# Cross attention in a transformer layer: where a tile's value products stand between two tiles' scores

## The chip, the core and the metric

The kernel runs on one core of a Trainium2 chip. The metric is the device time of one execution in microseconds (us). The core's engines are named as the profile names them: PE is TensorE (PEld its weight loads), DVE is VectorE, ACT is ScalarE, POOL is GpSimd, SP is SyncE, which issues the DMAs. Each engine runs its instructions in the order in which the program issues them, and waits on semaphores for the others.

## The reference, cut to what matters

One encoder layer over a short context (77 rows) and one decoder layer over 2048 rows, for two batches, width 512, 16 heads of 32. The change lies in the decoder's cross attention:

```
y = y + _mha(yn, yn, ...)                              # self attention over 2048 rows
q = _ln(y, n2) @ wq.T + bq                             # cross attention
scores = einsum('bhqd,bhkd->bhqk', q, k) / sqrt(hd) + bias
attn = softmax(scores, axis=-1)                        # 77 keys
out = einsum('bhqk,bhkd->bhqd', attn, v)               # the value products
y = y + out @ w_out.T + b_out
h = _ln(y, n3)
y = y + relu(h @ ff1.T + b1) @ ff2.T + b2              # feed-forward
```

All in float32.

## The kernel before, in words

The 2 x 2048 rows are cut into eight blocks of 512 rows, and each block into four tiles of 128 rows (`t` = 0 to 3). Self attention comes first, for all blocks, with the encoder and the cross attention of block 0 laid into it. Then come the feed-forward parts of the eight blocks; while block x is in its feed-forward part, block x + 1 goes through its cross attention. So seven cross attentions (`cross(x)`, line 1462, x = 1 to 7) run inside feed-forward parts, each with four tiles.

A feed-forward part has `per` = 56 slots. `ff_slot` (line 1439) is one slot's worth of it: in slots 0 to 27 a piece of the first product (`first_product`, line 1366, matmuls at line 1376), in slots 28 to 55 a piece of the second (`second_product`, line 1396, matmuls at line 1405). Both are Strassen-Winograd forms: seven products in place of eight, with sums of quarters made on DVE and POOL (`sums_h`, line 1333, which uses `half_sum`, line 1322, and `minus`, line 1112). `first_product` hands its result to DVE (line 1389, or to ACT at 1386) and then to ACT for the relu (line 1392).

The cross attention is a plan: a list of 56 lists of pieces, filled in `cross`. The main loop (lines 1659 to 1665) takes for each slot first the pieces of the plan, in the order in which they were put in the list (`next(side)`), and then `ff_slot`. The schedule is manual: the order on each engine is the order of the calls.

For tile t the plan has, counted from slot 13 + 5t, the stages of `attend_stages` (line 796):

- `score` (matmuls at line 808, +0): 16 small products, four heads in each of four PSUM banks, and behind them eight DVE operations, for each bank a maximum (line 817) and a subtraction (line 818);
- `exp` on ACT (line 821, +2), `sums` on DVE (lines 826, 827, +3), `normalize` on POOL (line 832, +3);
- `turned` (+7): four groups of transposes on PE (line 838), each into a bank of its own, and four copies on ACT (line 839) into `pts`;
- `times_v` (+10), the value products: 16 small matmuls into one bank (line 846) and a copy of that bank by ACT (line 850) into a buffer with the tag `xr`. For tiles 1 and 3 `sums_o` (line 1517) follows at once: three DVE operations, two of them in `minus` (line 1113) and one at line 1522, all of which read the bank of the products itself, and one on POOL.

So `times_v` of tile t falls on slot 23 + 5t, and `score` of tile t + 2 on slot 13 + 5(t + 2), the same one; in the list the products stand first, because the loop over t put them there first. That concerns t = 0 (slot 23) and t = 1 (slot 28); the products of tiles 2 and 3, in slots 33 and 38, meet no score.

The output products (`o_product`, line 1525, matmuls at line 1536) of tiles 0 and 1 lie in slots 31 to 34, those of tiles 2 and 3 in slots 40 to 43 (`O_SLOTS`); they read the copies and the sums. The norms behind them (`norm_stages`, line 759) start at slots 35, 36, 44 and 45, and their transposes (line 783) come four slots later.

PSUM has eight banks. In the feed-forward parts banks 4 to 7 belong to the feed-forward products; all pieces of the cross attention take banks 0 to 3 in a ring (`bank`, line 180, with `banks` = 4): whoever writes a bank waits until its last reader is done. The weights of the feed-forward and of the projections come by DMA through a ring of 16 tiles, filled by `feed` (line 1274) at each slot.

Of the kernel before, what the change touches and what calls it, by code (L numbers as in the profile page):

```python
# [54 lines left out]
def tile_encoder_decoder(ctx: ExitStack, tc: tile.TileContext, ins, out):  # L55
# [103 lines left out]
    with (  # L159
# [597 lines left out]
        def norm_stages(y, n, row, place, done):  # L757

            keep = {}

            def stats():
                st = sm.tile([P, 6], F32, name="bnst", tag="bnst")
                mv = sm.tile([P, 2], F32, name="cmv", tag="cmv", bufs=4)
                rs = sm.tile([P, 3], F32, name="crs", tag="crs", bufs=4)
                nc.vector.bn_stats(st, y())
                nc.vector.bn_aggr(mv, st)
                nc.vector.tensor_scalar_add(rs[:, 0:1], mv[:, 1:2], EPS)
                nc.gpsimd.tensor_tensor(rs[:, 1:2], rs[:, 0:1], mhalf[:, 0:1], ALU.pow)
                nc.gpsimd.tensor_scalar(rs[:, 2:3], mv[:, 0:1], rs[:, 1:2], -1.0, ALU.mult, ALU.mult)
                keep.update(rs=rs)  # L770

            def center():
                xn = keep["xn"] = place()
                rs = keep["rs"]
                nc.scalar.activation(xn, y(), AF.Identity, bias=rs[:, 2:3], scale=rs[:, 1:2])

            def add():
                nc.gpsimd.tensor_tensor(y(), y(), row, ALU.add)

            def turned():  # L780
                xn, pt, dst = keep["xn"], bank(), done()
                for c in range(NC):
                    nc.tensor.transpose(pt[:, ts(c, P)], xn[:, ts(c, P)], ident)  # L783
                for c in range(NC):
                    sc, bi = vec(f"dec_{n}_s", c), vec(f"dec_{n}_b", c)
                    nc.scalar.activation(dst[:, c, :], pt[:, ts(c, P)], AF.Identity, bias=bi, scale=sc)

            return stats, center, turned, add
# [272 lines left out]
        def y_of(x, t):  # L1061
            return ys[x % 3][:, t, :]
# [399 lines left out]
        def cross(x):  # L1462
# [4 lines left out]
            def place(tag):  # L1467
                if tag == "xr":
                    return lambda: sb.tile([P, D], F32, name=tag, tag=tag, bufs=2)
                return next_xt  # L1470

            for t in range(TB):
                fs = norm_stages(
                    lambda t=t: y_of(x, t), "n2", bv, place("xt"), lambda t=t: nT2[:, :, ts(t, P)]
                )
# [41 lines left out]
            def sums_o(t):  # L1517
                s = {n: of_o(t, n) for n in ("S1", "S2", "S3", "S4", "11", "12", "21")}
                a21, a22 = (held["o", t + 1]["bank"][:, ts(c, TOK)] for c in range(2))
                minus(ve, s["S3"], s["11"], a21)  # L1520
                minus(ve, s["S2"], a22, s["S3"])
                ve.tensor_tensor(s["S1"], s["21"], a22, ALU.add)
                minus(gp, s["S4"], s["12"], s["S2"])
# [36 lines left out]
            for t in range(TB):  # L1560
                at = 13 + 5 * t
                y = lambda t=t: y_of(x, t)
                biased = m == 0 and t < 2
                fs = attend_stages(
                    lambda g, t=t: qT[g // 2][:, g % 2, ts(t, P)], kTc, vc[0][:S, :], y, biased, prs[t % 2],
                    lambda g: pts_all[:S, g, :], place("xr"), wbt,
                    bias_1 if biased and t else None,
                )
                held["o", t] = fs[7]
                if t % 2:  # L1570
                    fs = fs[:5] + (lambda t=t, f=fs[5]: [f(), sums_o(t - 1)],)

                for k, f in zip((0, 2, 3, 3, 7, 10), fs):
                    plan[at + k].append(f)
                fs = norm_stages(y, "n3", bo, place("xt"), lambda t=t: nTt[:, :, ts(t, P)])
                at = (35, 36, 44, 45)[t]
                for k, f in zip((0, 2, 4), fs):
                    plan[at + k].append(f)
                rows_later[x * per + 15 + t] = fs[3]
# [60 lines left out]
        late_loads()  # L1640
        count.update(bank=0, banks=4)
        side = cross(1)
        slot(end)
        for s in range(4):
# [14 lines left out]
        for x in range(len(blocks)):  # L1659
            if x:  # L1660
                side = cross(x + 1) if x + 1 < len(blocks) else iter(())
            for n in range(per):
                if x or n >= 8:
                    next(side, None)
                    ff_slot(x * per + n)
# [37 lines left out]
```

## Time and profile before

| what | value |
|---|---|
| median of 3 runs | 2838.91 us (2832.11 to 2840.88) |
| the profiled execution, its own time | 2843.07 us |
| its span, from the first to the last instruction | 2841.2 us |
| mean granted PE clock | 0.989 |
| busy: PE, PEld, DVE, ACT, POOL | 98%, 74%, 65%, 50%, 31% of the span |
| HBM read, written | 309.51 MB, 41.49 MB |

The profile is of one execution. "Busy" is the time in which an engine has at least one instruction under way; matmuls are pipelined, so the end of one lies behind the start of the next, and the length of a group of them is best read from its start to the start of what follows. A float32 matmul shows as two records, so 16 products are x32. "Granted clock" is the share of full speed that PE was given in a stretch. `<-` in brackets names what ended an engine's idle time.

### The profile page before, as it was taken

How to read it: one execution, taken by the hardware profiler on the slowest of the kernel's cores; microseconds unless marked ns; L12 is line 12 of the kernel's file. 1: busy time of each engine (PE TensorE's matmuls, PEld its weight loads, DVE VectorE, ACT ScalarE, POOL GpSimd, SP SyncE). 2: the span in 40 equal slices, each digit the busy share in tenths (PEclk: the TensorE clock that was granted, in tenths of full speed). 3: DMA queues.
4: the chain of work that ended last, by engine and by line, in shares of the span. 5: the costliest groups of instructions: out<-in, count | busy, mean ns of one | idle time of the engine just before them, and what ended most of it. 6: DMA issues, size and time to landing. Idle time of an engine off the chain costs nothing. (4 is left out here: it accounts for less than half of the span.)

```text
span 2841.2 us, 65873 instructions
## 1 busy us (share of the span) xinstructions
PE 2790.7 (98%) x25998; PEld 2098.5 (74%) x25998; DVE 1857.5 (65%) x5360; ACT 1430.7 (50%) x2751; POOL 879.2 (31%) x745
## 2 busy tenths in 40 slices
PE   9999999999999999999999999999999999999998
PEld 5557666666666556666666677898989898989898
DVE  4666587778886577688788894646464645454545
ACT  3544466656665547665656674444434444434331
POOL 0301043300200303122100003364646464646456
PEclk9899999999999999999999999999999999999999
DMA  6414343401112512233301105464648464646475
GB/s 172 125 47 140 117 141 121 146 21 50 35 50 65 141 39 79 80 101 98 106 20 43 46 24 199 152 222 158 218 151 242 147 221 149 221 148 222 138 223 181
DMA packets 281270, 355.30 MB, mean 125 GB/s; under 512 B 37968, under 2 KB 156544, under 8 KB 280834
## 3 DMA queue, kind: packets, MB, share of 16 engines
q1 hardware_dynamic: 280962, 351.10, 39.9%
q8 instruction: 205, 3.36, 0.5%
q14 instruction: 103, 0.84, 0.1%
HBM read 309.51 MB, written 41.49 MB: 124 GB/s over the span
## 5 line engine op out<-in xcount | busy, mean ns | idle before, releaser
L404 ACT ACTIVATE pp<-pp,nm 128x128 f32<-128x128 f32 (+15 forms) x512 | 612.1, 1202 | 234.3 <-DVE nm L399 234.0
L382 DVE TENSOR_SCALAR_CACHE_REDUCE pp<-psum 128x512 f32<-128x512 f32 (+3 forms) x1024 | 559.4, 590 | 65.4 <-PE psum L373 63.6
L427 PEld LDWEIGHTS psum<-ident,pp 128*128 128x128 f32 x4352 | 472.2, 141 | 105.6 <-DVE pp L382 51.9
L427 PE MATMUL psum<-ident,pp 128*128 128x128 f32 x4352 | 533.1, 277 | 6.6 <-ACT pp L404 3.7
L433 ACT COPY pts<-psum 128x512 f32<-128x512 f32 (+3 forms) x592 | 297.0, 575 | 434.4 <-PE psum L427 304.6
L431 DVE COPY pts<-psum 128x512 f32<-128x512 f32 (+2 forms) x544 | 329.9, 659 | 66.1 <-PE psum L427 65.9
L373 PE MATMUL psum<-kT,q 32*128 32x512 f32 (+3 forms) x2560 | 358.8, 576 | 4.9 <-DVE pp L382 2.5
L444 PEld LDWEIGHTS psum<-pts,vv 128*32 128x32 f32 x8704 | 226.2, 110 | 124.7 <-issue 116.8
L1405 PE MATMUL psum<-pp 128*128 128x128 f32 x2560 | 306.7, 277 | 1.9 <-POOL pp L1113 1.6
L1405 PEld LDWEIGHTS psum<-pp 128*128 128x128 f32 x2560 | 299.2, 193 | 7.2 <-POOL pp L1113 2.1
L444 PE MATMUL psum<-pts,vv 128*32 128x128 f32 x8704 | 279.2, 275 | 0.7 <-ACT pts L433 0.5
L1113 POOL TENSOR_TENSOR pp<-pp 128x512 f32<-128x512 f32 x159 | 210.3, 1340 | 112.4 <-DMA pp<-in_dec_ff_wT_dram 50.9
L1376 PE MATMUL psum<-vv,pp 128*128 128x256 f32 x1024 | 243.6, 390 | 0.0
L373 PEld LDWEIGHTS psum<-kT,q 32*128 32x128 f32 x2560 | 124.0, 183 | 141.3 <-issue 91.2
L1376 PEld LDWEIGHTS psum<-vv,pp 128*128 128x128 f32 x1024 | 195.1, 195 | 27.7 <-issue 0.5
L389 DVE CUSTOM_DVE_ANT_0 pp<-psum,bias 128x256 f32<-128x256 f32 (+1 forms) x512 | 195.9, 411 | 16.7 <-PE psum L373 16.6
L1389 DVE TENSOR_TENSOR kT<-kT,psum 128x512 f32<-128x512 f32 x96 | 65.8, 687 | 190.3 <-PE psum L1376 190.1
L1392 ACT ACTIVATE kT<-kT,vecs 128x256 f32<-128x256 f32 x192 | 86.9, 500 | 173.7 <-DVE kT L1389 173.0
L1376 PE MATMUL psum<-nT,pp 128*128 128x256 f32 x768 | 173.9, 380 | 0.0
L286 POOL TENSOR_TENSOR rstd<-rstd,mhalf 128x1 f32<-128x1 f32 x32 | 18.5, 578 | 471.5 <-DVE rstd L285 368.9
L1376 PEld LDWEIGHTS psum<-nT,pp 128*128 128x128 f32 x768 | 145.6, 191 | 19.6 <-issue 0.2
L472 POOL TENSOR_TENSOR oT<-rirows,oT 128x512 f32<-128x512 f32 x30 | 38.7, 1289 | 360.9 <-DMA rirows<-rec 327.2
(207 smaller groups left out, 3816.8 us busy)
## 6 DMA issues: line engine op xcount, KB each, us to landing
pp<-w_d SPq DMA_DIRECT2D x520, 256.0 KB
pp<-in_dec_ff_wT_dram SPq DMA_DIRECT2D x112, 256.0 KB
wqk<-in_dec_sa_in_wT_dram SPq DMA_DIRECT2D x64, 256.0 KB
bias<-tzg SPq DMA_DIRECT2D x128, 128.0 KB
pp<-wo_d SPq DMA_DIRECT2D x56, 256.0 KB
wbig<-in_dec_sa_in_wT_dram SPq DMA_DIRECT2D x8, 1024.0 KB
vv<-in_enc_ff_wT_dram SPq DMA_DIRECT2D x8, 1024.0 KB
wbig<-in_dec_sa_out_wT_dram SPq DMA_DIRECT2D x8, 1024.0 KB
```

The source lines that it names most:

```text
L373: nc.tensor.matmul(banks[r][:, : kn * P], q[rows4(r), ts(t, P)], kT[rows4(r), g, k0 * P : (k0 + kn) * P], start=True, stop=True,)
L382: nc.vector.tensor_scalar(p[:, k0 * P : (k0 + far) * P], s[:, : far * P], 1.0, None, ALU.mult, ALU.max, accum_out=st["mx"][:, r, c : c + 1],)
L389: nc.vector.tensor_tensor_reduce(p[:, (i + 1) * P - w : (i + 1) * P], s[:, far * P : kn * P], biases[b, m, g][:, r, 2 * P - w :], 1.0, LOW ...
L404: nc.scalar.activation(p, p, AF.Exp, bias=nm, accum_out=to)
L427: nc.tensor.transpose(pt[:, ts(x, P)], state[n]["p"][r][:, ts(k, P)], ident)
L431: nc.vector.tensor_copy(pts[:, : len(load), :], pt[:, :w])
L433: nc.scalar.copy(pts[:, : len(load), :], pt[:, :w])
L444: nc.tensor.matmul(ot[rows4(r), t, :], vv[:, k, ts(g * HC + r, HD)], got.pop((n, k, r)), start=(k == 0), stop=(k == i),)
L1113: engine.tensor_tensor(out, a, b, ALU.subtract)
L1376: nc.tensor.matmul(mm[:, ts(f, TOK)], a[:, c, ts(f, P)], b[:, c, :], start=fresh and f == 0 and c == 0, stop=c == 1, skip_group_check=True,)
L1392: nc.scalar.activation(dst[:, e, :], src[:, e, :], AF.Relu, bias=vec("dec_ff1_b", f + e))
L1405: nc.tensor.matmul(psum[:, bank_i, ts(col, P)], lhs[:, c, :], w[:, c, :], start=fresh and k in (0, 3) and c == 0, stop=c == 3, skip_group_ ...
```

## The change

One number: the sixth stage of a tile (`times_v`, with `sums_o` behind it for odd tiles) is put 11 slots behind the tile's first one and not 10. It falls on slots 24, 29, 34 and 39. The score of tile t + 2 stays in slot 23 or 28 and now comes first; the feed-forward step of that slot lies between the two. In slot 34 the products come behind the last output product of tiles 0 and 1, in slot 39 behind the transposes of the first norm. The operations are the same, and so are their sizes.

```
-                for k, f in zip((0, 2, 3, 3, 7, 10), fs):
+                for k, f in zip((0, 2, 3, 3, 7, 11), fs):
                     plan[at + k].append(f)
```

## The prediction

> **What bounds the kernel now.** I read the page first, for the engine that fills the span.
>
> ```profile
> span 2841.2 us, 65873 instructions
> ## 1 busy us (share of the span) xinstructions
> PE 2790.7 (98%) x25998; PEld 2098.5 (74%) x25998; DVE 1857.5 (65%) x5360; ACT 1430.7 (50%) x2751; POOL 879.2 (31%) x745
> ```
>
> TensorE (PE) is busy for 98% of the span and no other engine comes near it, so a change gains only what it takes out of PE's own row: idle time, or time in which PE runs at a lower clock. The second view is the list of waits of PE, from 1600 us to the end, which holds all the feed-forward blocks that carry the cross attention of tiles 0 to 3.
>
> ```profile
> PE psum L808 <- DVE wqk L1522: 11.6, 7, 1.7
> PE psum L808 <- ACT xr L850: 6.2, 7, 0.9
> ```
>
> Columns: total us, times, longest. Both are waits of the score matmuls (L808): seven times for ScalarE's copy of a value product (L850), seven times for VectorE's last Strassen sum (L1522, in `sums_o`). No other row of that view reaches 2 us, and none names a DMA. To see why a score waits for a value product, the third view is the timeline of block 1, slots 22 to 25 and then 27 to 30. Columns: start us, length us, engine, line, operation, operands, count, and in brackets the idle time ahead of it.
>
> ```profile
> 1802.19 1.08 PE L846 MATMUL psum<-pts,q 77*32 77x128 f32 x32
> 1803.20 0.45 PE L808 MATMUL psum<-pts,bias 32*128 32x77 f32 x6
> 1804.52 1.11 PE L808 MATMUL psum<-pts,bias 32*128 32x77 f32 x26 [0.86 <-ACT xr L850]
> 1805.56 1.99 PE L1376 MATMUL psum<-vv,pp 128*128 128x256 f32 x8
> 1807.39 1.89 PE L1376 MATMUL psum<-nT,pp 128*128 128x256 f32 x8
> 1809.12 1.91 PE L838 MATMUL psum<-ident,pts 128*77 128x128 f32 x16
> 1810.87 1.89 PE L1376 MATMUL psum<-nT,pp 128*128 128x256 f32 x8
> ```
> ```profile
> 1803.90 0.56 ACT L850 COPY xr<-psum 128x512 f32<-128x512 f32 x1
> 1809.85 0.91 ACT L1392 ACTIVATE kT<-kT,vecs 128x256 f32<-128x256 f32 x2 [5.39 <-DVE kT L1389]
> ```
> ```profile
> 1806.05 0.48 DVE L818 TENSOR_TENSOR oT<-psum,cmx 128x308 f32<-128x308 f32 x1
> ```
> ```profile
> 1816.14 1.08 PE L846 MATMUL psum<-pts,q 77*32 77x128 f32 x32
> 1817.15 0.45 PE L808 MATMUL psum<-pts,bias 32*128 32x77 f32 x6
> 1819.26 1.08 PE L808 MATMUL psum<-pts,bias 32*128 32x77 f32 x26 [1.65 <-DVE wqk L1522]
> 1820.27 3.65 PE L1405 MATMUL psum<-pp,kT 128*128 128x128 f32 x16
> ```
> ```profile
> 1817.90 0.42 DVE L1113 TENSOR_TENSOR wqk<-xr,psum 128x256 f32<-128x256 f32 x1 [0.60 <-ACT xr L850]
> 1818.36 0.43 DVE L1113 TENSOR_TENSOR wqk<-psum,wqk 128x256 f32<-128x256 f32 x1
> 1818.70 0.41 DVE L1522 TENSOR_TENSOR wqk<-xr,psum 128x256 f32<-128x256 f32 x1
> ...
> 1823.87 1.89 DVE L1325 TENSOR_TENSOR pp<-kT 128x512 f32<-128x512 f32 x3
> ```
>
> The bank ring has four banks. A value product (L846) takes one, and the score directly behind it takes the next four, so the score's fourth bank is the product's own. Six records into the score, PE stops until that bank has been read: by one copy for an even tile (0.86 us idle), by the copy and three VectorE operations for an odd one (1.65 us). The full cost is from start to start: the score takes 1805.56 - 1803.20 = 2.36 us in slot 23 and 1820.27 - 1817.15 = 3.12 us in slot 28.
>
> The last row of PE shows a second loss: sixteen records of L1405 take 3.65 us there. Undisturbed steps stand in the next rows.
>
> ```profile
> 1780.66 1.13 PE L808 MATMUL psum<-pts,bias 32*128 32x77 f32 x32
> 1781.72 1.99 PE L1376 MATMUL psum<-vv,pp 128*128 128x256 f32 x8
> ```
> ```profile
> 1836.08 1.03 PE L1536 MATMUL psum<-wbig,wqk 128*128 128x256 f32 x4
> 1837.04 1.08 PE L846 MATMUL psum<-pts,q 77*32 77x128 f32 x32
> 1838.05 2.05 PE L1405 MATMUL psum<-pp 128*128 128x128 f32 x16
> 1839.94 1.03 PE L1536 MATMUL psum<-pp,xr 128*128 128x256 f32 x4
> 1840.80 1.95 PE L1405 MATMUL psum<-pp 128*128 128x128 f32 x16
> 1842.59 1.91 PE L838 MATMUL psum<-ident,pts 128*77 128x128 f32 x16
> ```
>
> Start to start, a score alone costs 1.06 us, a product alone 1.01, a first-layer step 1.73 (1807.39 to 1809.12) and a second-layer step 1.79 (1840.80 to 1842.59). A step behind small matrices costs 0.10 more (1805.56 to 1807.39 is 1.83; 1838.05 to 1839.94 is 1.89), one ahead of them 0.10 more too (1836.08 to 1837.04 is 0.96, against 0.86 for the like step from 1839.94 to 1840.80). So 3.65 for sixteen records that should take about 1.9 is a slow clock. A table by stretches shows it; the last columns are the granted clock, the DMA share and GB/s. First the last two and the sum of the ten windows at half the clock that lie between 1500 and 2830 us:
>
> ```profile
> 2533.63:2537.04 3.41, 3.41 (x19) 3.41 (x18) 3.31 (x9) 0.00 (x0) 0.00 (x0) 0.50 0.24 86
> 2659.92:2663.34 3.42, 3.42 (x10) 2.71 (x9) 3.28 (x8) 0.00 (x0) 0.00 (x0) 0.50 0.00 0
> sum 34.16, PE 34.16 PEld 30.71 DVE 31.96 ACT 0.00 POOL 1.07; mean PE 3.42 PEld 3.07 DVE 3.20 ACT 0.00 POOL 0.11
> ```
>
> PE is busy through all of it at 0.50, so half of 34.16, or 17.1 us, is lost: 1.71 us a window. Then the last and the sum of fourteen stretches, two for each of the seven blocks, each from the value product to the transposes (L838) two slots on, as from 1802.19 to 1809.12:
>
> ```profile
> 2671.74:2679.55 7.81, 6.16 (x98) 5.76 (x97) 4.88 (x13) 1.69 (x4) 4.16 (x3) 1.00 0.32 95
> sum 119.70, PE 101.94 PEld 90.66 DVE 79.95 ACT 26.19 POOL 38.51; mean PE 7.28 PEld 6.48 DVE 5.71 ACT 1.87 POOL 2.75
> ```
>
> All ten half-clock windows begin inside these stretches. What goes ahead of one is seen in the 3.41 us just before it. Here the PE busy time is that of the feed-forward matmuls alone:
>
> ```profile
> 2530.22:2533.63 3.41, 0.90 (x8) 0.90 (x9) 1.00 0.14 55
> 2673.58:2676.99 3.41, 1.12 (x10) 1.12 (x11) 1.00 0.12 42
> ```
>
> The first ends where the half-clock window from 2533.63 starts, and has 0.90 us of full-size matmuls, the most that any of the ten had ahead of it; the second, at the same place of the next block, has 1.12 and none follows. The rest is small matrices and waiting.
>
> **The change part by part.** What moves one slot is sixteen products (32 records, 1.01 us), the copy L850 and, for odd tiles, four sums; it issues no DMA, so SP's queue is passed by nothing, and nothing is added or removed. It is done for 28 products: four tiles, seven blocks.
>
> *Tiles 0 and 1.* The score now follows a feed-forward step, with its four banks long read, and costs 1.06. Slots 23 and 24 become score 1.06, step 23 at 1.73 + 0.10 + 0.10 = 1.93, product 1.01, step 24 at 1.83: 5.83 us. Slots 28 and 29: 1.06 + (1.79 + 0.20) + 1.01 + 1.89 = 5.95. The extra change between large and small matrices, 0.20 each time, is in that. Seven blocks: 7 x 11.78 = 82.5 us against 119.70, if all ten windows go: 37.2 saved, 17.1 of it clock and 20.1 waiting.
>
> *Tiles 2 and 3.* Their product has no score beside it. From 33 to 34 it stays behind an output product and ahead of a second-layer step; from 38 to 39 it passes the four transposes of a norm. Nothing, within one change of 0.1 us for each block, below or above.
>
> *New waits.* Three, on covers that I work out from block 1. (a) The product in slot 24 takes the score's first bank. VectorE had read that bank at 1806.53, 0.97 us after step 23 began at 1805.56; the product comes 1.93 after. Covered by 0.96. (b) The transposes of slot 25 take the product's bank for their fourth group. ScalarE's copy now stands behind the activation L1392 of slot 23, which waits for VectorE's L1389, which stands behind the score's eight operations. L1392 ends 1810.76 - 1805.56 = 5.20 us after step 23 began, the copy 5.76; the fourth group comes 1.93 + 1.01 + 1.83 and three quarters of 1.75 (1809.12 to 1810.87) later, 6.08 after. Covered by 0.3. Behind the copy on ScalarE stand L1392 of slot 24 and the copies of the turned tile, which PE needs four slots later. (c) In slot 29 the three VectorE sums stand behind the score's eight operations and two half sums (L1325). Those end at 1823.87 + 1.26 = 1825.13, the sums take 1819.11 - 1817.90 = 1.21, so 1826.34, or 6.07 after step 28 began; the fourth group of slot 30 comes 1.99 + 1.01 + 1.89 + 1.31 = 6.20 after. Covered by only 0.1. GpSimd's fourth sum falls behind the sum of slot 28, and is read four slots later. The cost of (a) to (c) is between nothing and 14 times the 1.30 us (2.36 - 1.06) that the 0.86 us wait costs today, 18.2; the covers hold, thinly, so I take 0.1 each, 1.4 us.
>
> Sum: 37.2 - 1.4 = 35.8 us. The profiled execution took 2843.07, 1.9 over its span: 2807.3. It lies 4.2 over the median of the runs, 2838.91; from that, 2803.1. The runs' scatter (2832.11 to 2840.88) is what five windows of 1.71 would make, so I can't say how many the median run had. I take the middle, **2805**.
>
> **The rivals.** (1) *The clock isn't the waits' doing.* Then the ten windows stay, only 20.1 - 1.4 = 18.7 is saved, and the time, counted from the middle of the two bases (2841) as in all that follows, is 2822. For it: PE's longest wait is 1.7 us, half of one window. Against it: all ten lie behind such waits and none elsewhere in seven blocks. The Trainium skill, "TensorE: Matmul & The Clock Gate", section "Why this matters for your kernels", warns of idle gaps over about 3 us and puts the fall of the clock at one window of idling; by that rule the waits here are too short, and this rival holds. The trace speaks against the rule: the window that starts at 1820.24 follows directly on 1.65 us of idle time.
>
> (2) *The wait moves.* Covers (b) and (c) fail by half a microsecond or so: with 1 us lost in each of the 14 stretches, and no half-clock windows, 37.2 - 14 = 23 saved: 2818.
>
> (3) *Slower: the clock falls at every separate piece.* Score and product are now 28 stretches of small matrices in place of 14. If each brought one window, 28 x 1.71 = 47.9 us is lost in place of 17.1, 30.8 more, and 18.7 is saved: 12 more than now, 2853. It decides from 10 + 18.7 / 1.71 = 21 windows on. For it: small matrices count for little in the windows above. Against it: scores alone at slots 13 and 18 and products alone at 33 and 38 occur 28 times in this trace with no half-clock window, and in the new order any 3.41 us have at least 3.41 - 1.75 = 1.66 us of large matmuls (beside the transposes), above the 1.12 that sufficed.
>
> (4) *Nothing:* the weights then come too late, and PE waits for DMA what it gained: 2839. Against it: PE never waits for a weight now.
>
> **How the numbers follow.** Forecast 2805, chance 0.72; rival 1, 0.07; rival 2, 0.09; rival 3, 0.08; rival 4, 0.04. A measurement can tell about 0.3% (8.5 us) from no change: faster 0.72 + 0.07 + 0.09 = 0.88, same 0.04, slower 0.08. The forecast's own range goes from 2797 (no new wait, 37.2 off the median, and 5 for the runs' scatter) to 2812 (0.5 us for each new wait); to hold 8 in 10 it takes in rival 2 at 2818 and ends at 2820.
>
> **What would show it.** Right: no score with idle time ahead of it, every score from start to start at 1.06 us, the two pairs of slots at 5.8 and 6.0 us, no half-clock window between 1500 us and the end of the last block. Wrong: PE idle ahead of the transposes L838 in slot 25 or 30, released by ACT L850 or DVE L1522 (rival 2); a clock of 0.50 in stretches where PE isn't idle (rivals 1 and 3); PE waiting for a weight's DMA (rival 4).

## The result, and the profile after

| | before | after |
|---|---|---|
| median, runs | 2836.72 us (2832.11 to 2840.88, 4 runs) | 2805.45 us (2804.72 to 2806.03, 4 runs) |
| profiled execution | 2843.07 us | 2804.72 us |
| span, mean granted PE clock | 2841.2 us, 0.989 | 2802.9 us, 0.995 |

The ratio is 0.989, with a 95% interval of 0.9873 to 0.9907: about 1.1% less time.

The page of the changed kernel, as far as it answers to the lines of before:

```profile
span 2802.9 us, 65879 instructions
## 1 busy us (share of the span) xinstructions
PE 2769.8 (99%) x25998; PEld 2079.2 (74%) x25998; DVE 1858.9 (66%) x5360; ACT 1430.6 (51%) x2751; POOL 875.4 (31%) x745
```

The counts of instructions of each engine are the same and so are the busy times of DVE, ACT and POOL, within 4 us. PE's busy time has fallen by 20.9 us with the same matmuls, which is what a faster clock looks like in this row (the ten half-clock windows of before make 17.1 of it); the idle time of PE has fallen from 50.4 to 33.1 us. The list of waits of PE from 1600 us on, by its first two rows:

```profile
PE psum L1405 <- POOL pp L1113: 1.6, 2, 1.2
PE psum L444 <- ACT pts L433: 0.5, 1, 0.5
```

Both rows of L808 are gone, and the longest entry that is left was there before. The timeline of PE, block 1, slots 23 to 25 and then 28 to 30:

```profile
1800.06 1.13 PE L808 MATMUL psum<-pts,bias 32*128 32x77 f32 x32
1801.12 1.99 PE L1376 MATMUL psum<-vv,pp 128*128 128x256 f32 x8
1803.05 1.08 PE L846 MATMUL psum<-pts,q 77*32 77x128 f32 x32
1804.06 1.99 PE L1376 MATMUL psum<-nT,pp 128*128 128x256 f32 x8
1805.89 1.91 PE L838 MATMUL psum<-ident,pts 128*77 128x128 f32 x16
...
1812.91 1.13 PE L808 MATMUL psum<-pts,bias 32*128 32x77 f32 x32
1813.97 2.05 PE L1405 MATMUL psum<-pp,kT 128*128 128x128 f32 x16
1815.95 1.08 PE L846 MATMUL psum<-pts,q 77*32 77x128 f32 x32
1816.96 2.05 PE L1405 MATMUL psum<-pp 128*128 128x128 f32 x16
1818.85 2.07 PE L838 MATMUL psum<-ident,oT 128*77 128x128 f32 x16
1820.76 1.95 PE L1405 MATMUL psum<-pp 128*128 128x128 f32 x16
```

The score goes through in one piece of 32 records (before: 6, a gap, 26) and takes 1.06 us from start to start in both slots. One thing is new: the transposes of slot 30 take 1820.76 - 1818.85 = 1.91 us, 0.16 more than their 1.75. Now the table by stretches, first the last row and the sum of the fourteen from score to transposes, then the whole of the feed-forward parts (the number behind the busy times is the granted clock):

```profile
2635.12:2641.06 5.94, 5.94 (x97) 5.54 (x97) 4.81 (x11) 1.69 (x4) 3.55 (x2) 1.00 0.49 162
sum 82.40, PE 82.40 PEld 72.54 DVE 69.80 ACT 20.18 POOL 31.45; mean PE 5.89 PEld 5.18 DVE 4.99 ACT 1.44 POOL 2.25
```
```profile
1500.00:2790.00 1290.00, 1286.15 (x11134) 1118.50 (x11134) 771.84 (x1702) 577.27 (x1121) 601.62 (x510) 1.00 0.53 170
```

The fourteen stretches take 82.40 us where they took 119.70, PE is busy in all of it, and none of the ten half-clock windows is left. (A 1.00 over 1290 us could hide one or two of them. Read in stretches of 60 us, each from 1500 to 2760 us has 1.00 too, where one window makes it 0.97, as from 2640 to 2700 us in the kernel before. The same holds of the long rows of this kind below.) From the first score of block 1 to the end the execution went from 2841.2 - 1780.66 = 1060.5 to 2802.9 - 1778.53 = 1024.4 us (the row of the start follows), 36.2 less; the other 2.1 us of the span were lost or won ahead of that, where the change has no part.

```profile
1778.53 1.13 PE L808 MATMUL psum<-pts,bias 32*128 32x77 f32 x32
```

### The profile page after: what moved, and what is told of

Its sections match the earlier page's. It is cut to its first block, busy times and chain, and to the rows that moved or that the text cites. A ratio compares the mean times of both kernels' runs of the same rounds, so it can differ in the third digit from the quotient of the medians.

```text
span 2802.9 us, 65879 instructions
## 1 busy us (share of the span) xinstructions
PE 2769.8 (99%) x25998; PEld 2079.2 (74%) x25998; DVE 1858.9 (66%) x5360; ACT 1430.6 (51%) x2751; POOL 875.4 (31%) x745
## 5 line engine op out<-in xcount | busy, mean ns | idle before, releaser
L1376 PE MATMUL psum<-vv,pp 128*128 128x256 f32 x1024 | 236.2, 381 | 0.0
```

The source lines that it names most:

```text
L1376: nc.tensor.matmul(mm[:, ts(f, TOK)], a[:, c, ts(f, P)], b[:, c, :], start=fresh and f == 0 and c == 0, stop=c == 1, skip_group_check=True,)
```

## The experiments

Theory W: the gain is the wait for a PSUM bank that the score asked for while it was still being read; the half-clock windows follow from these waits, because PE has too little to do. Rivals: A, the windows come from small matrices side by side, not from waiting; L, a slot more of time for the other engines is what helped, not the order. Times from the first score to the end ("tail") are worked out for each profile as above: before 1060.5, after 1024.4.

**Order alone, no later slot.** The products stay in slots 23 and 28, behind the score.

```
+            behind = []
...
-                for k, f in zip((0, 2, 3, 3, 7, 10), fs):
+                for k, f in zip((0, 2, 3, 3, 7), fs):
                     plan[at + k].append(f)
+                behind.append((at + 10, fs[5]))
...
+            for n, f in behind:
+                plan[n].append(f)
```

> The products stay in slots 23 and 28 but come behind the score of the tile two on. Theory W (what counts is that nobody on PE takes a bank whose reader has just been given its work; the half-clock windows follow from such waits): the product now takes the score's first bank, which VectorE frees about 1.07 us after it starts reading, so each of the 14 products waits about 1.0 us, released by VectorE L818. Stretches of about 1.06 + 1.1 + 1.01 + two steps, 6.8 to 7.0 us each, some half-clock windows (between 0 and 14, say 6): 2829 us, 2817 to 2838. Rival (the order alone is what helps, the slot between is idle detail): no wait, about 2803.

Measured: 2825.06 us, ratio 0.9955 (0.9941 to 0.9969). The waits of PE, and the sum of the half-clock windows behind 1500 us, of which there are four:

```profile
PE psum L846 <- DVE pts L818: 8.0, 7, 1.1
PE psum L846 <- DVE oT L818: 8.0, 7, 1.1
```
```profile
sum 13.66, PE 13.66 PEld 11.59 DVE 7.67 ACT 1.85 POOL 0.72; mean PE 3.42 PEld 2.90 DVE 1.92 ACT 0.46 POOL 0.18
```

The wait has changed sides: now the products ask for the score's first bank, and VectorE's subtraction has it for 1.1 us, as W expected. Order alone gives a part of the gain; the feed-forward step between the two gives the rest.

**A bank of their own.** Order and slots of before; the score of tiles 2 and 3 doesn't write the bank of the products (`HC` is 4, the number of its banks, so its 32 records become 24).

```
-        def attend_stages(q, kTc, v, y, biased, pr, pts, place, w_o, bi=None):
+        def attend_stages(q, kTc, v, y, biased, pr, pts, place, w_o, bi=None, heads=HC):
...
-                    for r in range(HC):
+                    for r in range(heads):
                         nc.tensor.matmul(
...
-                    s = banks[r][:, : NC * S].rearrange("p (g k) -> p g k", k=S)
+                    s = banks[r % heads][:, : NC * S].rearrange("p (g k) -> p g k", k=S)
...
-                    bias_1 if biased and t else None,
+                    bias_1 if biased and t else None, HC if t < 2 else HC - 1,
```

> Order and slots of before, but the scores of tiles 2 and 3 write only three of their four banks (a quarter of their heads isn't computed; VectorE reads the first bank in its place), so that the bank of the products isn't asked for. Theory W: no wait, no half-clock window, product and score side by side: 14 stretches of 1.01 + 1.0 + two steps, 5.6 and 5.7 us; one change between large and small matrices less than in the changed kernel, 14 x 0.2 = 2.8 us, and four products fewer in each score: 2801 us, 2798 to 2804. Rival A (the clock falls because product and score stand side by side): the waits go, the windows stay, 2801 + 17 = 2818. Rival L (only the later slot helps): as before, 2836.

Measured: 2812.02 us, ratio 0.9914 (0.989 to 0.9939), some 11 us over what W said. Its waits, and its feed-forward parts with the clock:

```profile
PE psum L838 <- DVE pts L818: 6.2, 7, 0.9
PE psum L838 <- DVE oT L818: 2.0, 7, 0.3
```
```profile
1500.00:2800.00 1300.00, 1286.93 (x11032) 1119.63 (x11031) 768.76 (x1704) 578.32 (x1121) 605.73 (x510) 1.00 0.56 169
```

No score waits and no window is left, with product and score side by side: that speaks for W and against A and L. Most of the miss has a cause of its own, made by the experiment: VectorE now reads the first bank a second time as its last, and the transposes two slots on wait for its L818, 8.2 us in all by the list. In block 1 the two stretches take 6.07 and 6.79 us where 5.6 and 5.7 were expected, which over seven blocks is 10.9 us; what the waits leave of it, some 2.7 us, lies in the steps and in the shortened score, which at 1.06 us costs as much as the whole one.

**The time kept, the idling filled.** Order and slots of before; PE gets matmuls without use while it would wait.

```
+            def fill(n):
+                for _ in range(n):
+                    nc.tensor.matmul(psum[:, count["bank"] % count["banks"], :P], ident, ident, start=True, stop=True)
...
+                if t >= 2:
+                    fs = (lambda t=t, f=fs[0]: [fill((4, 7)[t - 2]), f()],) + tuple(fs[1:])
```

> Order and slots of before; between the products and the score PE gets full-size matmuls with no use (4 of 128x128 behind tile 0, 7 behind tile 1; their result is overwritten by the score). Theory W, as to the clock: PE works through the time in which it waited, so nearly all idle time goes, the time itself does not (stretches of about 6.7 and 7.5 us), and no half-clock window is left: 2805.5 + 7 x (0.9 + 1.55) = 2823 us, 2819 to 2827. Rival A: the windows stay as they are before, about 10 of 1.71 us: 2840.

Measured: 2826.1 us, ratio 0.9963 (0.9949 to 0.9977). Two stretches, and the feed-forward parts:

```profile
1803.22:1810.15 6.93, 6.93 (x90) 6.08 (x90) 4.14 (x9) 1.38 (x3) 0.97 (x1) 1.00 0.27 81
```
```profile
2656.39:2664.20 7.81, 7.81 (x112) 7.40 (x112) 5.86 (x15) 1.96 (x6) 4.38 (x3) 1.00 0.32 102
sum 103.30, PE 103.30 PEld 94.44 DVE 69.97 ACT 23.34 POOL 37.30; mean PE 7.38 PEld 6.75 DVE 5.00 ACT 1.67 POOL 2.66
```
```profile
1500.00:2810.00 1310.00, 1305.60 (x11268) 1138.66 (x11266) 769.35 (x1703) 577.97 (x1123) 602.37 (x508) 1.00 0.55 168
```

Each stretch is as long as it was before without a window (6.93 to 6.96, and 7.80 or 7.81), only busy instead of idle, and all windows are gone. This is the clock's share by itself: 119.70 - 103.30 = 16.4 us. The other 20.9, from 103.30 to 82.40, are the waits. Against A this run says nothing, since the filler also stands between the product and the score; there the bank of their own decides.

**Both one slot later.** The scores of tiles 2 and 3 move with the products and stay behind them.

```
-                for k, f in zip((0, 2, 3, 3, 7, 10), fs):
+                for k, f in zip((t // 2, 2, 3, 3, 7, 11), fs):
```

> The products are one slot later as in the change, and the scores of tiles 2 and 3 too, so that products again stand directly in front of the scores, in slots 24 and 29. Theory W: the waits of before come back whole, with their windows: 2836 us, 2830 to 2842, and PE's waits are L808 for L850 and L1522, seven times each. Rival L (a slot more for the other engines is what helps): 2805.

Measured: 2864.96 us, ratio 1.0103 (1.0075 to 1.013): slower than before, which neither theory said. The waits of PE, then the half sums on VectorE and what GpSimd does meanwhile, in block 1:

```profile
PE psum L808 <- DVE wqk L1522: 22.8, 7, 4.0
PE psum L808 <- ACT xr L850: 6.0, 7, 0.9
```
```profile
1818.33 4.40 DVE L1325 TENSOR_TENSOR pp<-kT 128x512 f32<-128x512 f32 x2
```
```profile
1818.04 2.47 POOL L832 TENSOR_TENSOR oT<-oT,cri 128x1232 f32<-128x1232 f32 x1 [5.16 <-DVE cri L827]
1820.47 1.71 POOL L1113 TENSOR_TENSOR pp<-kT,pp 128x512 f32<-128x512 f32 x1
```

The same two waits are back, as W says, but in slot 29 the sums of the products stand behind the half sums of slot 28 on VectorE, and these two operations take 4.40 us where three took 1.89 before, beside GpSimd's: they end at 1821.06 and 1822.73 us, each 0.55 behind the end of one of GpSimd's two. The wait is 22.8 - 11.6 = 11.2 us longer, and there are 16 half-clock windows and not 10, 10.2 us more: together 21.4 (windows in which PE also waits count in both, a little), and the tail is 2862.9 - 1780.64 - 1060.5 = 21.8 longer. The Trainium skill, "SBUF — State Buffer", section "SBUF: two separate sides", says that VectorE with two SBUF inputs and GpSimd lock a pair of ports from each other for a whole instruction; these rows agree. L falls: one slot later, with the order kept, costs time.

**One tile alone.**

```
-                for k, f in zip((0, 2, 3, 3, 7, 10), fs):
+                for k, f in zip((0, 2, 3, 3, 7, 11 if t == 0 else 10), fs):
```

> Only tile 0's products go one slot later; tiles 1 to 3 stay as before. Theory W: the seven stretches of slots 23 and 24 go to 5.83 us without a window, those of slots 28 and 29 stay at 7.80 with the 1.65 us wait and some of their half-clock windows (0 to 7, say 5): 2805 + 7 x 1.85 + 5 x 1.71 - 1 = 2826 us, 2817 to 2830. If the two parts didn't add up (a gain of the one lost in the other), it would be at 2805 or at the time of before.

Measured: 2831.61 us, ratio 0.9982 (0.9965 to 1.0), just over the range given; the interval reaches to no change at all. The other one, with `t == 1` in the same place:

> Only tile 1's products, with their sums, go one slot later. Theory W: the stretches of slots 28 and 29 go to 5.94 us without a window; those of slots 23 and 24 stay at 6.93 to 6.96 with their wait of 0.86 us and some windows (0 to 7, say 4): 2805 + 7 x 1.1 + 4 x 1.71 = 2820 us, 2812 to 2825.

Measured: 2821.41 us, ratio 0.9939 (0.9917 to 0.996). In both profiles only the untouched tile's wait is left, with its 11.6 or 6.2 us. The windows are 9 with tile 0 moved (at two of seven places there are two in a row) and 5 with tile 1 moved; the last of these five are

```profile
2083.27:2086.68 3.41, 3.41 (x10) 2.70 (x9) 3.31 (x9) 0.00 (x0) 0.00 (x0) 0.50 0.03 8
2223.21:2226.63 3.42, 3.42 (x9) 2.73 (x9) 3.32 (x8) 0.00 (x0) 0.00 (x0) 0.50 0.00 0
2363.16:2366.57 3.41, 3.41 (x10) 2.70 (x9) 3.31 (x9) 0.00 (x0) 0.00 (x0) 0.50 0.14 8
```

With 1.71 us for each window taken off, the tails are 1043.5 before, 1035.4 and 1032.1 with one tile moved, 1024.4 with both: 8.1 and 11.4 saved, a sum of 19.5, and 19.1 together. So the waits add up, and in these profiled executions the windows don't: 10 become 9 or 5, and none where both waits go. How many windows there are differs from run to run, so these counts are draws: the mean clocks of the runs go from 0.989 to 0.992 with tile 0 moved, from 0.990 to 0.995 with tile 1 moved, and from 0.988 to 0.996 for the kernel before on the same chip.

**Tiles 2 and 3 alone.**

```
-                for k, f in zip((0, 2, 3, 3, 7, 10), fs):
+                for k, f in zip((0, 2, 3, 3, 7, 10 + t // 2), fs):
```

> Only the products of tiles 2 and 3, which meet no score, go one slot later. Theory W: nothing changes but the places: as the kernel before within 3 us. Rival L (a slot more for the other engines is what helps): half of the gain, some 15 to 18 us.

Measured: 2834.62 us, ratio 0.999 (0.9967 to 1.0012): no difference. The two rows of L808 are as before, and the tail of the profile is within 0.1 us of before's.

**Two slots later.** The products now stand directly in front of the next tile's transposes.

```
-                for k, f in zip((0, 2, 3, 3, 7, 10), fs):
+                for k, f in zip((0, 2, 3, 3, 7, 12), fs):
```

> All products two slots later than before, so that those of tiles 0 and 1 stand directly in front of the transposes of the next tile, whose fourth bank is the product's. Theory W: the wait is back in another place, PE L838 for ACT L850 (about 0.75 us, seven times) and for DVE L1522 (about 1.35 us, seven times): 2805 + 7 x (0.85 + 1.45) = 2821 us, 2815 to 2827, with no half-clock windows if transposes count as work of PE, and up to 14 x 1.71 = 24 us more if they don't. Rival L: 2805 or less.

Measured: 2822.31 us, ratio 0.9943 (0.9927 to 0.996). The waits, and one of the places:

```profile
PE psum L838 <- DVE wqk L1522: 6.5, 7, 0.9
PE psum L838 <- ACT xr L850: 6.4, 7, 0.9
```
```profile
2654.97 1.08 PE L846 MATMUL psum<-pts,q 77*32 77x128 f32 x32
2655.98 1.53 PE L838 MATMUL psum<-ident,oT 128*77 128x128 f32 x12
2658.45 0.63 PE L838 MATMUL psum<-ident,oT 128*77 128x128 f32 x4 [0.94 <-DVE wqk L1522]
2658.92 1.95 PE L1405 MATMUL psum<-pp 128*128 128x128 f32 x16
```

As W said, the wait sits at the fourth group, twelve records in; the longest is 0.9 us for both kinds, where 0.75 and 1.35 were expected. So the place in between has limits on both sides: one slot earlier the score waits, one later the transposes do. The fourteen stretches of some 3.95 us hold products, transposes and a wait and nothing else, and the clock stays at 1.00 from 1500 to 2800 us, which speaks for the transposes counting as work of PE here.

**The last wait taken away.** The changed kernel, with tile 2's transposes at the front of slot 31; and the changed kernel again, on the same chip.

```
+                if t == 2:
+                    plan[at + 8].insert(0, fs[4])
+                    fs = fs[:4] + (lambda: None,) + fs[5:]
```

> The changed kernel, with tile 2's transposes moved from slot 30 to the front of slot 31, so that the bank that they take from tile 1's products has one more feed-forward step to come free. Theory W: the last wait of the new order (0.15 us, seven times, PE L838 behind DVE L1522) goes, nothing else moves: 1.1 us less than the changed kernel, 2804.4 where that one takes 2805.5, a difference that only the trace can show. If the later transposes made the products of tile 2 or the output products wait, it would be slower by 1 us or more.

> The changed kernel again, on the chip of this call, to compare with. As measured: 2805.5 us, 2804 to 2807, with no half-clock window behind 1500 us, so its runs lie within 2 us of each other, where those of the kernel before lie some 20 us apart.

Measured: 2805.53 us (ratio 0.9889, 0.9873 to 0.9906) and 2806.34 us (0.989, 0.9873 to 0.9908). The times can't tell them apart. In the traces the wait of the weight loads that the second one shows is gone from the first (why it is put down to the sums, though the row names ScalarE's copy, stands in the next section):

```profile
PEld psum L838 <- ACT pts L839: 1.2, 7, 0.2
```

and the tails are 2800.8 - 1777.62 = 1023.2 and 2800.7 - 1776.40 = 1024.3: 1.1 us, as expected. The runs of the changed kernel lay 6.4 us apart here and not 2 as I had written; those of the kernel before, beside them, 18. The slower ones of the changed kernel have a lower mean clock (0.994 against 0.997); where in the run that falls is not known, since only the fastest of the five has a trace.

## Why the prediction was right, point by point

- **What bounds it, and the two losses.** Right. The stretches were forecast at 82.5 us and took 82.40; the score takes its 1.06, and the steps ahead of and behind the products (1.93 and 1.98, 1.83 and 1.89 by the rows above) lie within 0.01 of what the rows of before gave.
- **The clock.** Right: ten windows were to go and ten went. The bank of their own shows that product and score side by side don't bring them, and the filled wait that none comes when PE works through the same time. Rival 1 falls. So does the rule that it rests on, if idling means a whole window without any matmul: waits of 1.1 us were enough in the kernel with the order alone. But idle time alone doesn't bring a window either: the kernel with two slots has waits of 0.9 us among transposes and no window. Two readings of the prediction were off. The window from 1820.24 us doesn't follow directly on the idle time: 0.98 us of score matmuls lie between (1819.26 to 1820.24). And the full-size matmuls in the 3.41 us ahead don't decide by themselves: the stretch in the row below, again with the feed-forward matmuls alone, has 0.54 us, and one from 1956.78 has 0.86, and no window follows either, though one follows 0.90.

```profile
1943.12:1946.53 3.41, 0.54 (x3) 0.14 (x1) 1.00 0.45 142
```

- **The new waits.** (a) held: the first bank was free when the products came. (b) held, by 0.2 us in place of 0.3: the copy ended 5.85 us after the step began. (c) did not quite: the sums end at 1819.73 + 0.41 = 1820.14, the row below, 6.17 us after the step began at 1813.97 and not 6.07; and PE goes on some 0.15 us after the last sum (1819.11 to 1819.26 in the kernel before), which the cover of 0.1 left out. So the transposes' fourth group waits 0.16 us in all seven blocks. That is the 1.1 us that the last experiment takes away, against 1.4 put down for all three. The list of waits names ScalarE's first copy of the transposes (L839), which ends at about the same time; but in slot 25 all four groups are through by 1807.63, before the first such copy begins at 1807.69, so they don't need it.

```profile
1819.73 0.41 DVE L1522 TENSOR_TENSOR wqk<-xr,psum 128x256 f32<-128x256 f32 x1
```

- **The sum.** 35.8 us forecast, 36.2 in the tail of the profiled executions, 31.3 between the medians (33.5 from the median of three runs that the prediction had). The term that doesn't fit the medians is the clock's: the profiled execution of before had ten windows, its median run, by its time, fewer. The runs of the kernel before that stood beside the experiments (19, 29 and 11 on three chips) lie between 2824.78 us, at a mean clock of 0.996, and 2845.68, at 0.988, so this kernel has no single number of windows. Its fastest run has about the mean clock of the changed kernel (0.995) and lies 19.3 us over it, which is near the 20.1 us forecast for the waits alone; the kernel with the wait filled, 20.7 us over it, says the same. The prediction counted from the middle of two bases and came out at 2805 for that reason, not by a better one.
- **Rivals 2 to 4.** None took place. Rival 2 is what the kernel with two slots has; rival 3 would have needed more than 20 windows and there is none; no row names a weight's DMA.

## What to carry to other kernels

In a ring of PSUM banks, ask for every piece which bank it will get and who read that bank last; a piece that needs the whole ring must not come right behind a piece that still has to be evacuated, and one step of other work between the two was enough here, where the step behind it hardly ran into the same bank. Price a wait of PE from start to start and by the granted clock around it: here 18 us of idle time in the list of waits were 36 us in the profiled executions. When the same change is tried by halves, the clock's share need not split as the waits do, and it differs from run to run.

## What the runs showed of the hardware

- A half-clock window costs PE about 1.71 us and lasts 3.41; with tile 0 moved, two came in a row at two places. In the trace of before, from 1500 us on, one came only where the 3.41 us ahead of it had 0.90 us of full-size matmuls or less, but not always there (0.54 and 0.86 were once followed by none), and none where they had 1.03 or more. What else decides stays open. It takes no long gap: waits of 0.86 to 1.65 us did it, where small matrices stood on either side.
- The windows lie on a grid of 3.413 us: with tile 1 moved they come at 2083.27, 2223.21 and 2363.16 us, 139.95 apart, or 41 windows, and in the kernel before, at the waits of tile 1 from 2103.55 us on, 143.36 apart, or 42. The blocks nearly keep step with it: in the kernel before, the products of tile 1 start 143.14 us apart in the last blocks (2385.46 and 2528.60), so each block meets the grid some 0.2 us earlier than the one ahead of it. So a wait is met again and again, until it has moved too far: the 0.90 us of full-size matmuls in one block are 1.12 in the next, and no window follows.
- VectorE's half sums of 128x512 beside GpSimd's work took 4.40 us for two, against about 0.63 each without it. A VectorE operation that PE waits for should not stand behind them.
